# The reset gate of a GRU by seven products, with shared products added up in one PSUM bank, in a four-layer graph network

## The chip, the cores and the metric

The kernel runs on one core of one Trainium2 chip. The metric is the device time of one execution in microseconds, smaller is better. In the text PE is TensorE (the matrix engine), DVE is VectorE, ACT is ScalarE, POOL is GpSimd, and SP is SyncE, which here only issues DMAs.

## The reference, cut to what matters

The input is `x`, 128 graphs of 128 nodes with 256 features in float32, and `adj`, an integer adjacency matrix for each graph. Four layers follow one another; after each, the layer's result is added to its input and normalised over the features.

- Layer 0 is attention: four scores `(x*a_k) @ x.T`, of which `adj == k+1` picks one for each pair of nodes, a softmax, and the product with `x`.
- Layer 1 sends messages: `relu(x @ W_upd + mean over neighbours of x @ W_msg + bias)`.
- Layer 2 is a gated recurrent unit that runs three steps. This is the layer that the change concerns:

```python
m = h @ weight[i]; aggr = A.T @ m
gi = aggr @ w_ih.T + b_ih
gh = h @ w_hh.T + b_hh
r = sigmoid(i_r + h_r)            # reset gate
z = sigmoid(i_z + h_z)            # update gate
n = tanh(i_n + r * h_n)           # candidate
h = (1 - z) * n + z * h
```

- Layer 3 is attention again, with a score `f_i + f_j`, a mask `adj > 0`, a softmax and an ELU.

## The kernel before

**Tiling.** Four graphs make a group (`G = 4`), so there are 32 groups, and a tile has 128 partitions by 512 columns (four graphs of 128 nodes). The hidden state is kept transposed, in two halves `hT[0]` and `hT[1]` of 128 features each. `weight[i] @ w_ih.T` is multiplied out once, at the start, into `c_gi[:, i]`, so that a step first sums the neighbours (`aggregate`, on three bfloat16 parts of `h`), copies that to `agT`, and then multiplies by `c_gi` and `w_hhT`.

**Products of a gate.** A gate has 256 output features, 256 input features and 512 columns, from two sources (`h` with `w_hhT`, and `agT` with `c_gi`). Taken as 2 by 2 blocks it is eight block products of 256 columns for each source. `direct` does it plainly: for each half of the output, two matmuls of 512 columns for each source, all four added up in one bank. This is how the reset gate is made (lines 769 to 772), and `reset` takes its tanh from the bank. The update gate uses the seven products of the Strassen-Winograd scheme: `sums` prepares four differences of the state's blocks (`t_h` on GpSimd, `t_m` on VectorE), `w_s` holds three sums of the weights' blocks, and `seven` issues the seven products of 256 columns of a source. They lie in four banks,

```python
BANKS = ((1, 6), (5, 7), (4,), (3, 2))
```

and `gate` (line 708) adds them up into the four quarters of the tile `t_z` when all are done: one ScalarE copy, six VectorE additions, and a tanh for each half. `seven(of_h, ...)` comes ahead of `seven(of_m, ...)`, so that the products of `h` can run while the neighbours are still being summed, and the same holds for the first `direct` of each reset half.

**Order of the work.** No engine's order is written by hand. Every call is recorded as an `Op`, and a planner at the end (from line 905) issues the operations in the order of a list schedule: of those that could start first on an engine it takes the one with the smallest due time `nominal`. The due times come from `paced`, which spreads the operations of a layer over a stretch of `PERIOD` for each group; `SPAN = 2` means that the three GRU steps of a group take two periods, so two groups are always in the GRU while others are in layers 0, 1 and 3. What an operation costs the planner is in `pe_cost`, `dve_cost`, `act_cost` and `pool_cost`, what a hand-over between engines costs in `HOP`, `PE_HOP` and `SLACK`, and a landing DMA in `LANDING`. `urgent` operations (the GRU's) get `EAGER` ahead on engines other than PE. The order is fixed when the kernel is built; on the chip every engine goes through its queue in order and waits for semaphores.

**Buffers.** PSUM has four banks under the tag `ps` and four under `gate`. `t_z` and `t_h` are one buffer each, `q` and `m_gt` have three and four, `hn` (the new state turned back) has four.

**Masks and scaled inputs.** Layer 0's `prepared(k)` makes the mask `mk` on VectorE (line 534), and the scaled input `xs` for the scores half on GpSimd (line 539), half on ScalarE (line 541). Layer 1 makes `m_gt` and `a_ne` on VectorE (lines 590 to 593). Line 231, which the profile shows everywhere, is the planner's own `issue`.

Of the kernel before, what the change touches and what calls it, by code (L numbers as in the profile page):

```python
# [9 lines left out]
U8 = mybir.dt.uint8  # L10
# [8 lines left out]
def kernel(  # L19
# [135 lines left out]
    class Op:  # L155
        def __init__(self, engine):
            self.engine, self.calls, self.took, self.landing = engine, [], 0.0, 0.0
            self.after, self.bufs, self.waiting = {}, [], 0
            self.ready, self.nominal, self.urgent = 0.0, 0.0, False
            self.waits = self.holds = False  # L160

    class Engine:
        def __init__(self, name, engine, cost):
# [71 lines left out]

    LANDING = 3.8
    HOP = 0.3
    PE_HOP = 1.0  # L240
    SLACK = 1.0

    def pe_cost(op, n, sums):
        return 0.11 if op == "transpose" else 0.222 if n <= P else n / 600.0

    SPLIT = 0.056

# [51 lines left out]

    w3x = tile_of("w3x", [P, KC, 2 + D])  # L300

    w_s = tile_of("w_s", [P, NL + 1, 3, P])

    def weights():

# [2 lines left out]
        for src, tag, bufs in ((w_ih, "hT", 6), (w_hh, "rest", 4)):  # L308
            for g in range(0, NGC, 2):
                nat = tile_of(tag, [P, 2, D], bufs)  # L310
                ACT.dma_start(out=nat, in_=src[g * P : (g + 2) * P].rearrange("(g p) d -> p g d", p=P))
                nats.append(nat)
            if src is w_ih:
                for i in range(NL):
                    w = tile_of("hn", [P, KC, D], 4)
# [62 lines left out]
        for n in range(NL + 1):  # L378
            by = POOL if n > 1 else DVE
            w = [  # L380
                (w_hhT[:, k] if n == 0 else c_gi[:, n - 1, k])[:, (KC + e) * P : (KC + e + 1) * P]
                for e in range(2) for k in range(KC)
            ]
            a11, a12, a21, a22 = w
# [134 lines left out]
    def layer0(g, s):  # L519
# [11 lines left out]

        def prepared(k):
            mk = tile_of("mk", [P, G, N], 2, U8)
            DVE.tensor_scalar(mk, a_f, float(k + 1), None, op0=OP.is_equal)
            xs = []
            for c in range(KC):
                t = tile_of("xs", [P, T], 2)
                if c == 0:
                    POOL.tensor_scalar(t, xT[c], acol[:, k, c : c + 1], None, op0=OP.mult)
                else:  # L540
                    ACT.mul(t, xT[c], acol[:, k, c : c + 1])
                xs.append(t)
            return mk, xs

# [94 lines left out]
    def gru(g, s):  # L639
# [5 lines left out]
        def step(i, hT, parts):  # L645
# [31 lines left out]
            def sums(by, v, w, n, src, tag):  # L677


                t = tile_of(tag, [P, 4, H])  # L680
                b11, b12, b21, b22 = v[0][:, :H], v[0][:, H:], v[1][:, :H], v[1][:, H:]
                s12, s21, s22 = src[0][:, H:], src[1][:, :H], src[1][:, H:]
                by.tensor_sub(t[:, 0], s12, b11)
                by.tensor_sub(t[:, 2], s22, b12)
                by.tensor_sub(t[:, 1], s22, t[:, 0])
                by.tensor_sub(t[:, 3], s21, t[:, 1])
                block = lambda k, e: w[:, k, (Z + e) * P : (Z + e + 1) * P]
                return {
                    1: (block(0, 0), b11), 2: (block(1, 0), b21), 3: (w_s[:, n, 2], b22),
                    4: (block(1, 1), t[:, 3]), 5: (block(0, 1), t[:, 0]),  # L690
                    6: (w_s[:, n, 0], t[:, 1]), 7: (w_s[:, n, 1], t[:, 2]),
                }

            BANKS = ((1, 6), (5, 7), (4,), (3, 2))

            def seven(of, banks, first, last):

                for j, numbers in enumerate(BANKS):
                    if first:
                        banks.append(bank("gate"))  # L700
# [7 lines left out]
            def gate(tag, q, banks):  # L708

                t = tile_of(tag, [P, 4, H])  # L710
                b16, b57, b4, b32 = [b.rearrange("p (h n) -> p h n", [P, 2, H], h=2) for b in banks]
                ACT.copy(t[:, 0], b16[:, 0])
                DVE.tensor_add(t[:, 3], b16[:, 1], t[:, 0])
                DVE.tensor_add(t[:, 1:3], b57, t[:, 3:4].to_broadcast([P, 2, H]))
                DVE.tensor_add(t[:, 3], b57[:, 0], t[:, 2])
                DVE.tensor_add(t[:, 2], b4[:, 0], t[:, 2])
                z = [t[:, 2 * c : 2 * c + 2].rearrange("p h n -> p (h n)") for c in range(KC)]
                ACT.activation(z[1], z[1], AF.Tanh, bias=brz[:, q + 1 : q + 2], scale=0.5)
                DVE.tensor_add(t[:, 1], b32[:, 0], t[:, 1])
                DVE.tensor_add(t[:, 0], b32[:, 1], t[:, 0])  # L720
                ACT.activation(z[0], z[0], AF.Tanh, bias=brz[:, q : q + 1], scale=0.5)
                return z

            def hidden(c, ps):
                t = tile_of("q", [P, T], 3)
                ACT.activation(t, ps, AF.Identity, bias=bhn[:, c : c + 1], scale=0.5)
                return t

            def reset(c, ps):
                t = tile_of("t_r", [P, T], 2)  # L730
                ACT.activation(t, ps, AF.Tanh, bias=brz[:, c : c + 1], scale=0.5)
                return t

            def candidate(c, ps, t, q):
# [8 lines left out]
            def update(c, z, n, d):  # L743

                DVE.scalar_tensor_tensor(d, z, 1.0, d, op0=OP.add, op1=OP.mult)
                new[c] = tile_of("hT", [P, T], 6)
                DVE.scalar_tensor_tensor(new[c], d, 0.5, n, op0=OP.mult, op1=OP.add)
                turning[c] = tile_of("hn", [P, G, P], 4)
                flat = turning[c].rearrange(FLAT)
                if g == NG - 1 and i == NL - 1:  # L750
                    turned_quick(flat, [new[c][:, b * N : (b + 1) * N] for b in range(G)])
                else:
                    back(flat, turned(new[c].rearrange("p (b n) -> p b n", b=G), G, "h"))
                if i < NL - 1:
                    split_up[c] = split(turning[c], DVE)
# [131 lines left out]
    for g in range(NG):  # L887
        s = State()
        loading(g, s)
        layer0(g, s)  # L890
        paced(g - 2.0, g - 1.0)
        layer1(g, s)
        paced(g - 1.0, g - 0.05)
        gru(g, s)
        if g < NG - 1:
            layer3(g, s, 0, G)
            paced(g + SPAN + 0.05, g + SPAN + 1.0)
        else:

            for b in range(0, G, 2):  # L900
                layer3(g, s, b, b + 2)
                paced(g + SPAN + 0.05, g + SPAN + 1.0)


    order = {}
# [18 lines left out]
    def take_slot(buf):  # L924
# [6 lines left out]
    EAGER = 10.0  # L931

    def start_of(op):

# [21 lines left out]
    while left:  # L956
        best = None
        for e in engines:
# [5 lines left out]
            if best is None or at < best[0]:  # L964
                op = min(
                    (op for t, op in starts if t <= at),
                    key=lambda op: op.nominal - (EAGER if op.urgent and e is not PE else 0.0),
                )
                best = (at, op)
        at, op = best  # L970
# [50 lines left out]
```

## Time and profile before

| | |
|---|---|
| time, median of 3 runs | 2891.55 us (2890.46 to 2894.75) |
| profiled execution, span | 2889.2 us |
| PE busy | 2820.4 us, 98% |
| weight loads busy | 1814.3 us, 63% |
| DVE busy | 2418.6 us, 84% |
| ACT busy | 1277.3 us, 44% |
| POOL busy | 1293.8 us, 45% |
| mean granted TensorE clock | 0.992 |

A float32 matmul shows in the profile as two records, a bfloat16 one as one. Matmuls are pipelined: a record's end is modelled and lies beyond the start of the next, so the time that a matmul costs is read from the distance between starts. A name such as `gate<-agT,c_gi` says that a tile of the tag `gate` is written from `agT` and `c_gi`. Times in the timeline are from the start of the span.

### The profile page before, as it was taken

To read this page: it belongs to the slowest core of one execution; us is meant where nothing else is said; L and a number is where in the kernel's file an instruction comes from. 1 tells how busy PE (TensorE), PEld (TensorE's weight loads), DVE (VectorE), ACT (ScalarE), POOL (GpSimd) and SP (SyncE) were. 2 spreads that over 40 slices of the span, in tenths; PEclk is the share of its full clock that TensorE was granted. 3 is DMA by queue.
4 is the path that set the end of the run, shared out by engine and by line. 5 is a ranking of instruction groups with operands and counts; after the bars stand their busy time and mean duration, and the time that the engine had idled before them with its cause. 6 is when DMAs were issued, how large, how long until landed. Compare 5 with 4: busy or idle time off the path is not lost.

```text
span 2889.2 us, 39658 instructions
## 1 busy us (share of the span) xinstructions
PE 2820.4 (98%) x12028; PEld 1814.3 (63%) x12028; DVE 2418.6 (84%) x5549; ACT 1277.3 (44%) x2712; POOL 1293.8 (45%) x1326
## 2 busy tenths in 40 slices
PE   7799999999999999999999999999999999999996
PEld 5566666666666666666666666666666666666563
DVE  5778898888888888898888888888898888888876
ACT  3234444444444444444444444444444443444444
POOL 3434545444455444445434454444444434454432
PEclk9999999999999999999999999999999999999997
DMA  5434565555555555565555555555555555544542
GB/s 112 109 83 85 125 130 104 123 106 110 124 128 112 105 117 107 124 130 105 117 112 109 124 126 109 110 114 113 124 125 110 110 113 110 127 110 97 106 92 55
DMA packets 1396612, 321.58 MB, mean 111 GB/s; under 512 B 1142064, under 2 KB 1387952, under 8 KB 1396400
## 3 DMA queue, kind: packets, MB, share of 16 engines
q1 hardware_dynamic: 1393952, 316.69, 52.2%
q10 hardware_dynamic: 2448, 2.36, 0.3%
q8 instruction: 97, 1.59, 0.2%
q14 instruction: 115, 0.94, 0.1%
HBM read 185.74 MB, written 133.15 MB: 110 GB/s over the span
## 4 chain that ended last, share of the span: by engine, by line
PE 86%; DVE 8%; issue 3%; ACT 1%; DMA 1%; POOL 1%; SPq 0%; ACTq 0%; DVEq 0%; POOLq 0%
PE ps L231 48%; PE gate L231 38%; DVE hT L231 1%; DVE t_z L231 1%; DVE t_r L231 1%; DVE rest L231 1%; DVE t_m L231 1%; DVE st L231 1%; DVE mk L231 0%; DVE z L231 0%; DVE xd L231 0%; ACT agT L231 0%; DVE z_h L231 0%; DVE t_d L231 0%; SPq L231 0%
## 5 line engine op out<-in xcount | busy, mean ns | idle before, releaser
L231 PE MATMUL gate<-agT,c_gi 128*128 128x512 f32 (+1 forms) x1152 | 470.2, 524 | 2.7 <-ACT agT L231 2.7
L231 POOL TENSOR_TENSOR rstd<-rstd,neg_half 128x4 f32<-128x4 f32 (+1 forms) x128 | 144.7, 1131 | 512.9 <-DVE rstd L231 510.3
L231 PE MATMUL ps<-agT,c_gi 128*128 128x512 f32 x768 | 355.3, 592 | 0.0
L231 DVE TENSOR_TENSOR t_z<-gate,t_z 128x256 f32<-128x256 f32 x576 | 254.4, 460 | 86.2 <-ACT t_z L231 65.5
L231 PEld LDWEIGHTS gate<-agT,c_gi 128*128 128x128 f32 x1152 | 218.4, 191 | 160.0 <-issue 136.9
L231 PE MATMUL gate<-hT,w_hhT 128*128 128x512 f32 (+1 forms) x768 | 316.9, 530 | 0.2 <-DVE t_z L231 0.2
L231 POOL TENSOR_SCALAR xs<-xT,acol 128x512 f32<-128x512 f32 x128 | 210.3, 1643 | 205.5 <-PE ps L231 175.9
L231 PEld LDWEIGHTS ps<-xs,xT 128*128 128x128 f32 x2048 | 249.7, 193 | 66.7 <-issue 54.1
L231 PE MATMUL ps<-xs,xT 128*128 128x128 f32 x2048 | 251.5, 276 | 10.4 <-POOL xs L231 10.4
L231 ACT ACTIVATE t_n<-t_r,bih 128x512 f32<-128x512 f32 x192 | 138.0, 719 | 274.1 <-DVE t_r L231 263.3
L231 PEld LDWEIGHTS ps<-agT,c_gi 128*128 128x128 f32 x768 | 145.8, 190 | 157.4 <-issue 146.9
L231 PE MATMUL ps<-hT,w_hhT 128*128 128x512 f32 x512 | 240.8, 593 | 0.0
L231 PE MATMUL ps<-w_um,x1T 128*128 128x512 f32 x512 | 235.1, 592 | 1.9 <-ACT x1T L231 1.9
L231 ACT ACTIVATE t_r<-gate,brz 128x512 f32<-128x512 f32 x192 | 130.0, 685 | 237.5 <-PE gate L231 237.4
L231 ACT ACTIVATE t_z<-t_z,brz 128x512 f32<-128x512 f32 x192 | 131.4, 714 | 223.3 <-DVE t_z L231 220.6
L231 POOL TENSOR_TENSOR t_d<-hT,t_n 128x512 f32<-128x512 f32 x128 | 172.5, 1352 | 108.9 <-ACT t_n L231 107.3
L231 DVE TENSOR_TENSOR t_r<-t_r,ps 128x512 f32<-128x512 f32 x192 | 131.4, 685 | 98.5 <-PE ps L231 90.7
L231 POOL TENSOR_TENSOR t_d<-h0T,t_n 128x512 f32<-128x512 f32 x64 | 92.7, 1448 | 266.0 <-ACT t_n L231 266.0
L231 ACT ACTIVATE q<-ps,bhn 128x512 f32<-128x512 f32 x192 | 130.9, 682 | 173.2 <-PE ps L231 173.1
L231 PEld LDWEIGHTS gate<-hT,w_hhT 128*128 128x128 f32 x768 | 141.5, 192 | 104.5 <-issue 98.5
L231 PEld LDWEIGHTS ps<-hT,w_hhT 128*128 128x128 f32 x512 | 97.6, 191 | 108.4 <-issue 103.4
L231 ACT COPY agT<-ps 128x512 f32<-128x512 f32 x192 | 109.1, 587 | 118.7 <-PE ps L231 111.2
(191 smaller groups left out, 6249.2 us busy)
## 6 DMA issues: line engine op xcount, KB each, us to landing
way_h<-z_h SPq DMA_DIRECT2D x190, 256.0 KB, 2.4
hn<-way_h SPq DMA_DIRECT2D x760, 64.0 KB, 2.4
x_blocks<-in_x_dram SPq DMA_DIRECT2D x256, 64.0 KB, 2.3
x_in<-in_x_dram SPq DMA_DIRECT2D x32, 512.0 KB, 3.8
way_x<-xb SPq DMA_DIRECT2D x32, 512.0 KB, 3.1
way<-z SPq DMA_DIRECT2D x64, 256.0 KB, 2.5
way_p<-z_p SPq DMA_DIRECT2D x62, 256.0 KB, 2.4
probT<-way_p SPq DMA_DIRECT2D x248, 64.0 KB, 2.4
```

Source lines behind the costliest of these rows:

```text
L231: getattr(self.engine, name)(*[a.real() if isinstance(a, View) else a for a in args], **{k: a.real() if isinstance(a, View) else a for k, ...
```

## The change

The reset gate is also made from seven products of each source, with the same `t_h` and `t_m` that the update gate uses; `w_s` gets a second block of weight sums for it. `seven`, `BANKS` and the old `gate` go, and a new `gate` serves both. In it products that several quarters of the output have in common add up in one bank, `shared`: product 1, then 6, then 7, then 4. Between them ScalarE copies the bank's sum so far into a quarter of the gate's tile (`snapshot`), and the next product goes on adding to the same bank. Products 2, and then 5 and 3, lie in two other banks, and VectorE adds these to the copied quarters (`plus`); the last sum is taken by the tanh straight from the bank. Each product is added for both sources at once. A snapshot has a planner bonus of its own, `rush`.

Besides, the masks `mk` and `m_gt` go from VectorE to GpSimd, both halves of `xs` are made on ScalarE, some tiles have fewer buffers, and the planner's numbers are set anew.

```diff
-    LANDING = 3.8
+    LANDING = 4.2
...
-        return 0.11 if op == "transpose" else 0.222 if n <= P else n / 600.0
+        return 0.11 if op == "transpose" else 0.222 if n <= P else 0.003 + n / 599.0
...
-        return 0.55 if op == "memset" else 1.2 if n < 64 else 0.25 + n * 0.0023
+        return 1.56 if op in FAST else 0.55 if op == "memset" else 1.2 if n < 64 else 0.25 + n * 0.0023
...
-    PERIOD = 88.0
+    PERIOD = 92.637
     SPAN = 2.0
-    H_END, M_START, M_END = 0.25, 0.22, 0.60
+    EAGER, RUSH = 21.446, 39.26
+    L0_START, L0_END, L1_START, L1_END, L3_START, L3_END = -2.0, -1.338, -0.867, -0.05, 0.05, 1.0
+    H_END, M_START, M_END = 0.25, 0.12, 0.573
...
-    w_s = tile_of("w_s", [P, NL + 1, 3, P])
+    w_s = tile_of("w_s", [P, NL + 1, 3, 2, P])
...
             mk = tile_of("mk", [P, G, N], 2, U8)
-            DVE.tensor_scalar(mk, a_f, float(k + 1), None, op0=OP.is_equal)
+            POOL.tensor_scalar(mk, a_f, float(k + 1), None, op0=OP.is_equal)
...
-                if c == 0:
-                    POOL.tensor_scalar(t, xT[c], acol[:, k, c : c + 1], None, op0=OP.mult)
-                else:
-                    ACT.mul(t, xT[c], acol[:, k, c : c + 1])
+                ACT.mul(t, xT[c], acol[:, k, c : c + 1])
...
-        s.m_gt = tile_of("m_gt", [P, G, N], 4, U8)
-        DVE.tensor_scalar(s.m_gt, a_f, 0.0, None, op0=OP.is_gt)
+        s.m_gt = tile_of("m_gt", [P, G, N], 3, U8)
+        POOL.tensor_scalar(s.m_gt, a_f, 0.0, None, op0=OP.is_gt)
...
+            def gate(tag, q, sources):
+                t = tile_of(tag, [P, 4, H])
+                shared, other, last = bank("gate"), bank("gate"), bank("gate")
+
+                def add(ps, p, first=False):
                     with PE:
-                        for k, p in enumerate(numbers):
+                        for k, of in enumerate(sources):
                             PE.matmul(
-                                banks[j][:, k * H : (k + 1) * H], *of[p],
-                                start=(first and k == 0), stop=(last and k == len(numbers) - 1),
+                                ps[:, :H], *of(q)[p], start=(first and k == 0),
+                                stop=(p in (2, 3, 4) and k == len(sources) - 1), skip_group_check=True,
                             )
...
+                def snapshot(quarter):
+                    ACT.copy(t[:, quarter], shared[:, :H])
+                    ops[-1].rush = RUSH
+
+                def plus(quarter, ps):
+                    DVE.tensor_add(t[:, quarter], ps[:, :H], t[:, quarter])
+
+                def tanh(out, in_, c):
+                    ACT.activation(out, in_, AF.Tanh, bias=brz[:, q + c : q + c + 1], scale=0.5)
+
+                add(shared, 1, True)
+                snapshot(0)
+                add(last, 2, True)
+                plus(0, last)
+                add(shared, 6)
+                snapshot(1)
+                add(other, 5, True)
+                add(shared, 7)
+                snapshot(3)
+                plus(3, other)
+                tanh(t[:, 3], t[:, 3], 1)
+                add(shared, 4)
+                tanh(t[:, 2], shared[:, :H], 1)
+                add(other, 3)
+                plus(1, other)
+                halves = [t[:, 2 * c : 2 * c + 2].rearrange("p h n -> p (h n)") for c in range(KC)]
+                tanh(halves[0], halves[0], 0)
+                return halves[1], halves[0]
...
-                t = tile_of("q", [P, T], 3)
+                t = tile_of("q", [P, T], 2)
...
-                turning[c] = tile_of("hn", [P, G, P], 4)
+                turning[c] = tile_of("hn", [P, G, P], 3)
...
-            r0 = direct(w_hhT, hT, R, stop=False)
-            t0 = reset(0, direct(w_i, agT, R, r0))
-            r1 = direct(w_hhT, hT, R + 1, stop=False)
-            t1 = reset(1, direct(w_i, agT, R + 1, r1))
+            t1, t0 = gate("t_r", R, (of_h, of_m))
+            n1, d1 = candidate(1, direct(w_i, agT, C + 1), t1, q1)
             n0, d0 = candidate(0, direct(w_i, agT, C), t0, q0)
-            n1, d1 = candidate(1, direct(w_i, agT, C + 1), t1, q1)
-            z_banks = []
-            seven(of_h, z_banks, True, False)
-            seven(of_m, z_banks, False, True)
-            z = gate("t_z", Z, z_banks)
-            update(1, z[1], n1, d1)
-            update(0, z[0], n0, d0)
+            z1, z0 = gate("t_z", Z, (of_h, of_m))
+            update(1, z1, n1, d1)
+            update(0, z0, n0, d0)
```

More of the change, by code (lines that the diff above doesn't have):

```diff
@@ L160, in __init__ @@
             self.waits = self.holds = False
+            self.rush = 0.0
     class Engine:
@@ L314, in weights @@
                 for i in range(NL):
-                    w = tile_of("hn", [P, KC, D], 4)
+                    w = tile_of("hn", [P, KC, D], 3)
                     ACT.dma_start(out=w, in_=weight[i].rearrange("(c p) e -> p c e", p=P))
@@ L380, in weights @@
             w = [
-                (w_hhT[:, k] if n == 0 else c_gi[:, n - 1, k])[:, (KC + e) * P : (KC + e + 1) * P]
-                for e in range(2) for k in range(KC)
+                (w_hhT[:, k] if n == 0 else c_gi[:, n - 1, k])[:, : 4 * P].rearrange(
+                    "p (g e x) -> p g e x", [P, 2, 2, P], g=2, e=2
+                )
+                for k in range(KC)
             ]
-            a11, a12, a21, a22 = w
+            a11, a12, a21, a22 = w[0][:, :, 0], w[1][:, :, 0], w[0][:, :, 1], w[1][:, :, 1]
             s2, s3, s4 = [w_s[:, n, j] for j in range(3)]
@@ L686, in sums, with of @@
                 by.tensor_sub(t[:, 3], s21, t[:, 1])
[L687 to L700, printed above, removed]
+                def of(q):
+                    block = lambda k, e: w[:, k, (q + e) * P : (q + e + 1) * P]
+                    extra = lambda j: w_s[:, n, j, q // KC]
+                    return {
+                        1: (block(0, 0), b11), 2: (block(1, 0), b21), 3: (extra(2), b22),
+                        4: (block(1, 1), t[:, 3]), 5: (block(0, 1), t[:, 0]),
+                        6: (extra(0), t[:, 1]), 7: (extra(1), t[:, 2]),
+                    }
@@ L701, in seven @@
+                return of
+            def gate(tag, q, sources):
+                t = tile_of(tag, [P, 4, H])
+                shared, other, last = bank("gate"), bank("gate"), bank("gate")
+                def add(ps, p, first=False):
                     with PE:
-                        for k, p in enumerate(numbers):
+                        for k, of in enumerate(sources):
                             PE.matmul(
-                                banks[j][:, k * H : (k + 1) * H], *of[p],
-                                start=(first and k == 0), stop=(last and k == len(numbers) - 1),
-                            )
@@ L708, in gate @@
[L708 to L722, printed above, removed]
+                                ps[:, :H], *of(q)[p], start=(first and k == 0),
@@ L724, in hidden @@
+                halves = [t[:, 2 * c : 2 * c + 2].rearrange("p h n -> p (h n)") for c in range(KC)]
+                tanh(halves[0], halves[0], 0)
+                return halves[1], halves[0]
             def hidden(c, ps):
-                t = tile_of("q", [P, T], 3)
+                t = tile_of("q", [P, T], 2)
                 ACT.activation(t, ps, AF.Identity, bias=bhn[:, c : c + 1], scale=0.5)
[L727 to L731, printed above, removed]
@@ L890 @@
         layer0(g, s)
-        paced(g - 2.0, g - 1.0)
+        paced(g + L0_START, g + L0_END)
         layer1(g, s)
-        paced(g - 1.0, g - 0.05)
+        paced(g + L1_START, g + L1_END)
         gru(g, s)
@@ L896 @@
             layer3(g, s, 0, G)
-            paced(g + SPAN + 0.05, g + SPAN + 1.0)
+            paced(g + SPAN + L3_START, g + SPAN + L3_END)
         else:
@@ L901 @@
                 layer3(g, s, b, b + 2)
-                paced(g + SPAN + 0.05, g + SPAN + 1.0)
+                paced(g + SPAN + L3_START, g + SPAN + L3_END)
     order = {}
@@ L929, in take_slot @@
         taken.append(buf)
-    EAGER = 10.0
     def start_of(op):
@@ L966 @@
                     (op for t, op in starts if t <= at),
-                    key=lambda op: op.nominal - (EAGER if op.urgent and e is not PE else 0.0),
+                    key=lambda op: op.nominal - (EAGER if op.urgent and e is not PE else 0.0) - op.rush,
                 )
```

## The prediction

> **What bounds the kernel now.** I read the page's busy times first, then the chain that ended last, then the groups kept apart by shape, and last two stretches of the timeline.
>
> ```profile
> PE 2820.4 (98%) x12028; PEld 1814.3 (63%) x12028; DVE 2418.6 (84%) x5549; ACT 1277.3 (44%) x2712; POOL 1293.8 (45%) x1326
> PEclk9999999999999999999999999999999999999997
> PE 86%; DVE 8%; issue 3%; ACT 1%; DMA 1%; POOL 1%; SPq 0%; ACTq 0%; DVEq 0%; POOLq 0%
> ```
>
> PE is busy for 98% and is 86% of the chain. A busy PE can still be badly fed, so I check the spacing of its starts. In the middle of the run:
>
> ```profile
> 1401.75 1.88 PE L231 MATMUL ps<-hT,w_hhT 128*128 128x512 f32 x4
> 1403.46 1.95 PE L231 MATMUL ps<-xs,xT 128*128 128x128 f32 x16
> ...
> 1406.98 0.59 PE L231 MATMUL gate<-agT,c_gi 128*128 128x256 f32 x2
> 1407.41 0.59 PE L231 MATMUL gate<-t_m,w_s 128*128 128x256 f32 x2
> 1407.84 0.59 PE L231 MATMUL gate<-t_m,c_gi 128*128 128x256 f32 x2
> ...
> 1408.04 0.37 ACT L231 COPY t_z<-gate 128x256 f32<-128x256 f32 x1 [3.69 <-PE gate L231]
> ```
>
> Four records of 512 columns take 1403.46 - 1401.75 = 1.71 us; two records are a matmul, so 0.857 us each. A 256-column matmul takes 0.432 us (the steps 1406.98, 1407.41, 1407.84). Nothing lies between: PE streams. Between 90 and 2800 us it is busy 2689.47 of 2710.00 us in the windows view, and the waits that the trace names there come to some 30 us. So PE's own work is the time, and a matmul removed is worth its spacing unless PE begins to wait.
>
> **The skill.** The Trainium skill, "TensorE: Matmul & The Clock Gate", Back-to-back issue gap, gives N/2.4 + 2.5 ns. For 512 columns that is 216 ns; a float32 record is spaced 0.429 us, twice that, and a 256-column record 0.216 us, half of it. The trace agrees that halving the columns costs next to nothing extra. "PSUM — Partial Sum Buffer", The four PSUM rules, says that hardware allows a synchronised read of a partial sum in the middle of an accumulation group. No run so far shows it; before, every bank is read after its last product. "Perfetto Trace Analysis", Matmuls, advises that independent groups rotate through banks so that eviction overlaps the next matmuls. The shared bank does the opposite for products 6, 7 and 4, which is where a new wait could come from.
>
> **TensorE, part by part.** The reset gate was 8 matmuls of 512 columns a step: 8 x 0.857 = 6.86 us. It becomes 14 of 256: 14 x 0.432 = 6.05 us. There are 32 x 3 = 96 steps: 96 x 0.81 = 78 us off PE. The update gate keeps its 14 products, and aggregation, candidate and layers keep theirs. In the built order I count 7202 matmuls before and 7778 after, which is 96 x 6 more, as it should be.
>
> **The new wait: a shared bank between PE and ACT.** Products 6, 7 and 4 of each gate must wait until ACT has copied the bank: 3 x 2 x 96 = 576 hand-overs. Their latency can be read from before:
>
> ```profile
> 2837.34 0.28 PE L231 MATMUL ps<-a_ne,rest 128*128 128x128 bf16 x2
> 2837.65 1.07 ACT L231 COPY agT<-ps 128x512 f32<-128x512 f32 x2 [0.65 <-PE ps L231]
> 2838.29 1.13 PE L231 MATMUL gate<-agT,c_gi 128*128 128x512 f32 x2 [0.68 <-ACT agT L231]
> ```
>
> ACT starts 0.03 us after PE's modelled end, and PE starts 0.06 us after a copy of 0.58 us. For a 256-column product the end lies 0.16 us beyond the next start (0.379 against 0.216), so a hand-over needs 0.16 + 0.03 + 0.37 + 0.06 = 0.63 us of other PE work in between. I gave each matmul of the built order its spacing and summed what stands between the products of one shared bank: the median is 3.4 us before products 6 and 7 and 1.7 us before product 4. Only 3 of 576 stand with nothing between, and 13 more with 0.85 us. If ACT is prompt, this costs 3 x 0.63, about 2 us. ACT is not always prompt: behind a tanh that waits for DVE the snapshot is late, PE stops, and everything queued behind that product on PE stops with it. Before product 4 the margin is 1.7 - 0.63 = 1.1 us, one and a half ACT instructions of 0.7 us. I take 4 us in all for this, a guess between 2 and the 40 of the rival below.
>
> **The other engines.**
>
> ```profile
> L231 POOL TENSOR_SCALAR xs<-xT,acol 128x512 f32<-128x512 f32 x128 | 210.3, 1643 | 205.5 <-PE ps L231 175.9 <-DMA acol<-in_L_gnn_a_dram 11.8 <-DVE xT L231 9.8
> L231 DVE TENSOR_TENSOR t_z<-gate,t_z 128x256 f32<-128x256 f32 x480 | 188.3, 414 | 77.6 <-ACT t_z L231 65.5 <-PE gate L231 7.1 <-DVE t_z L231 0.5
> L231 DVE TENSOR_TENSOR t_z<-gate,t_z 128x512 f32<-128x512 f32 x96 | 66.2, 689 | 8.6 <-PE gate L231 0.4
> L231 DVE TENSOR_SCALAR mk<-a_f 128x512 uint8<-128x512 f32 x128 | 72.7, 571 | 1.1
> L231 DVE TENSOR_SCALAR m_gt<-a_f 128x512 uint8<-128x512 f32 x32 | 19.0, 594 | 1.4 <-POOL a_f L231 1.4
> L231 ACT ACTIVATE xs<-xT,acol 128x512 f32<-128x512 f32 x128 | 92.5, 723 | 109.4 <-PE ps L231 101.8 <-DVE xT L231 4.0 <-DVE fac L231 2.1
> L231 ACT COPY t_z<-gate 128x256 f32<-128x256 f32 x96 | 35.4, 369 | 206.2 <-PE gate L231 206.2
> ```
>
> DVE loses the masks, 72.7 + 19.0 us, and the gate additions go from 188.3 + 66.2 to 6 x 96 x 0.414 = 238 us: 2418.6 - 91.7 - 16 = 2311 us. ACT gains 128 more xs at 0.723 = 93 us, five more copies a step at 0.369 = 177 us, and a tanh of 512 columns becomes two of 256 in each of 192 gates. A 256-column tanh is not shown; the copy's 0.37 us and the 0.59 us of a 256-column scaled activation from SBUF bound it, and with 0.70 for 512 columns that is 192 x 0.04 to 192 x 0.48, or 8 to 92 us. I take 45: 1277 + 93 + 177 + 45 = 1592 us. POOL loses 210 us of xs and gains 160 masks. The trace has no mask on POOL. The skill's "GPSIMD Engine Reference", Elementwise — side-by-side cycle accounting, gives 769 ns for 512 elements, but the nearest row, also a TENSOR_SCALAR of 128x512, takes 1.643 us; I take the row, 263 us: 1294 - 210 + 263 = 1347 us, or 1207 at the page's price. In a span of 2823 us these are 82, 56 and 48%. All stay below PE, whose work hides them; PE waits for xs (10.4 us before) may fall a little, as ACT makes both halves in 1.45 us where POOL took 1.64 for one. I cost that at nothing: ACT also evicts the weights at that time. The doubled weight sums are 16 instructions once, beside PE's own 30 us of preparation. The planner's numbers and fewer buffers only move order; I cost them at nothing and leave their risk to the range.
>
> **The end.** Before, the products of h for both gates run while the last step waits for its state to come back through DRAM (PE is on them from 2824.56 to 2832.68). Now each product takes both sources at once, so all 28 stand behind the last aggregation. PE work from there: before 8 x 0.857 + 10 x 0.432 = 11.2 us, after 28 x 0.432 + 4 x 0.857 = 15.5 us, 4.3 more. Snapshots with little else queued add some 2 to 3 us, a shorter tail of additions gives 1 back. I take 6 us. In the middle of the run other groups' work fills those waits.
>
> **Sum.** 2891.5 - 78 + 4 + 6 = 2823.5, say 2823 us.
>
> **Rivals.**
> - Late snapshots. For it: ACT goes from 44 to 56% busy, in order, with waits for DVE ahead of copies. Against: the distances above, and PE waited only 7 us in all for agT copies. If a fifth of 576 hand-overs is late by 0.35 us, that is 40 us: 2859 us.
> - Slower than before. If each gate holds PE 0.5 us, through the hand-overs and a single t_r buffer together, 192 x 0.5 = 96 us: 2819 + 96 = 2915 us. The distances speak against it; a planner that is off under the new load would be for it.
> - Faster still. DVE is 108 us lighter, and PE's waits for DVE and POOL in the middle (rest 9, t_r 7, hT 5, xs 10 us) halve: 2823 - 15 = 2808 us.
> - No change: the 68 us just eaten up. Nothing points to that number.
>
> **How the numbers follow.** Forecast 0.61, late snapshots 0.20, faster still 0.12, slower 0.05, no change 0.02. The range is from just below the third rival, 2803, to just above the first, 2862, which leaves out the last two and the outer part of the others. Faster by over 0.2% is 0.61 + 0.20 + 0.12 = 0.93, same 0.01 (half of the last case), slower 0.06.
>
> **What would show it.** Right: 256-column gate matmuls still spaced 0.432 us, PE busy near 2740 us, PE's waits for ACT t_r and t_z together under 10 us, last gate matmul to the end of the span near 40 us as before. Wrong: PE idle before gate groups released by ACT t_r or t_z in tens of us, or POOL rows for mk above 2 us with DVE's alpha waiting for them.

## The result, and the profile after

The changed kernel takes 2804.52 us (median of 4 runs, 2800.18 to 2806.17); runs of the kernel before beside it gave 2893.15 us (4 runs, 2890.46 to 2895.49). The ratio is 0.9692, interval 0.9675 to 0.9708: 88.6 us less. The two profiled spans, 2889.2 and 2802.0 us, differ by 87.2 us. The forecast was 2823 us, 18.5 us too high, inside its range of 2803 to 2862.

The page of the changed kernel, busy times, the granted clock in 40 slices, and the chain that ended last by engine:

```profile
span 2802.0 us, 42709 instructions
...
PE 2741.4 (98%) x13180; PEld 2030.5 (72%) x13180; DVE 2351.3 (84%) x5389; ACT 1552.1 (55%) x3512; POOL 1349.1 (48%) x1358
...
PEclk9999999999999999999999999999999999999996
...
PE 95%; DVE 2%; ACT 1%; issue 1%; DMA 0%; POOL 0%; ACTq 0%; POOLq 0%; DVEq 0%
```

PE executes 1152 records more (two for each of 96 x 6 matmuls) and is busy 79 us less. Its share of the chain went from 86 to 95%: no wait has taken the place of the work that went. The timeline of a reset gate in the changed kernel (start, duration, engine, form, and in brackets the idle time before and who ended it):

```profile
1408.14 0.59 PE L232 MATMUL gate<-h0T,w_hhT 128*128 128x256 f32 x2
1408.58 0.59 PE L232 MATMUL gate<-agT,c_gi 128*128 128x256 f32 x2
1409.01 0.59 PE L232 MATMUL gate<-t_h,w_hhT 128*128 128x256 f32 x2
1409.44 0.59 PE L232 MATMUL gate<-t_m,c_gi 128*128 128x256 f32 x2
1409.47 0.36 ACT L232 COPY t_r<-gate 128x256 f32<-128x256 f32 x1
...
1416.32 0.59 PE L232 MATMUL gate<-t_m,w_s 128*128 128x256 f32 x2
1416.75 1.95 PE L232 MATMUL ps<-xs,xT 128*128 128x128 f32 x16
1416.95 0.37 ACT L232 COPY t_r<-gate 128x256 f32<-128x256 f32 x1 [1.04 <-PE gate L232]
1418.53 0.60 PE L232 MATMUL gate<-t_h,w_s 128*128 128x256 f32 x2
1418.96 0.59 PE L232 MATMUL gate<-t_m,w_s 128*128 128x256 f32 x2
```

The 256-column matmuls still start 0.43 us apart (1408.14, 1408.58, 1409.01, 1409.44). The sum is copied out in its middle: the product that ends at 1416.91 is copied at 1416.95, and the next one goes into the same bank at 1418.53. Between them PE does layer 0's scores (`ps<-xs,xT`), so it does not stand still. This is the read of an open accumulation that "PSUM — Partial Sum Buffer", The four PSUM rules, of the Trainium skill allows; the trace now shows 576 of them.

The view of PE's waits in the changed kernel (who waits and for what: us in all, times, longest):

```profile
PE ps L232 <- ACT wh L232: 10.8, 2, 10.0
PE ps L232 <- ACT prob L232: 6.5, 2, 4.2
PE ps L232 <- DVE hT L232: 4.8, 2, 2.9
...
PE ps L232 <- DVE rest L232: 4.5, 5, 1.8
PE gate L232 <- DVE t_z L232: 3.2, 3, 1.8
...
PE ps L232 <- ACT xs L232: 2.3, 3, 1.4
...
PE gate L232 <- ACT t_z L232: 1.4, 3, 0.5
```

The same view of the kernel before:

```profile
PE ps L231 <- POOL xs L231: 10.4, 6, 2.8
...
PE ps L231 <- DVE rest L231: 6.4, 15, 1.9
PE ps L231 <- DVE t_r L231: 5.2, 13, 0.7
```

The snapshots show there with 1.4 us (ACT `t_z`, three waits), and not at all for `t_r`. The view counts from the modelled end of the record before; from start to start the same three waits cost 1.9 us, as is worked out further down. The waits for `xs` fall from 10.4 to 2.3 us, those for DVE `t_r` vanish.

**Where 87.2 us come from.** I gave each PE record the distance that its kind has to the next when nothing is waited for (0.429 us for 512 float32 columns, 0.216 for 256, 0.1115 for 128, 0.056 for 128 in bfloat16) and put what is over in the distances between starts down as waits, apart for the first 180 us, the last 100 us and what lies between. The waits so hold more than idle time: where the granted clock falls to 0.50, as it does in parts of the first 180 and the last 100 us, records start up to twice as far apart, and that is in them too (about 6 and 7 us in the outer columns before, 5 and 8 us after). Sums in us:

| kernel | work | waits, first 180 | waits, middle | waits, last 100 | span |
|---|---|---|---|---|---|
| before | 2777.7 | 45.9 | 27.5 | 38.2 | 2889.2 |
| after | 2699.3 | 35.0 | 21.4 | 46.2 | 2802.0 |
| difference | -78.4 | -10.9 | -6.1 | +8.0 | -87.2 |

So the work fell as forecast; the waits fell by 9 where the forecast had them rise by 10. The same sums for every run below stand at the end of the experiments.

### The profile page after: what moved, and what is told of

Read it like the earlier page. It is cut to its first block, busy times and chain, and to the rows that moved or that the text cites. A ratio compares the mean times of both kernels' runs of the same rounds, so it can differ in the third digit from the quotient of the medians.

```text
span 2802.0 us, 42709 instructions
## 1 busy us (share of the span) xinstructions
PE 2741.4 (98%) x13180; PEld 2030.5 (72%) x13180; DVE 2351.3 (84%) x5389; ACT 1552.1 (55%) x3512; POOL 1349.1 (48%) x1358
## 4 chain that ended last, share of the span: by engine, by line
PE 95%; DVE 2%; ACT 1%; issue 1%; DMA 0%; POOL 0%; ACTq 0%; POOLq 0%; DVEq 0%
PE ps L232 54%; PE gate L232 41%; DVE t_r L232 0%; DVE rest L232 0%; DVE t_d L232 0%; ACT xs L232 0%; DMA acol<-in_L_gnn_a_dram 0%; DMA hn<-in_L_gnn_weight_dram 0%; ACT ps L232 0%; DVE xd L232 0%; POOL mk L232 0%; DVE hT L232 0%; DVE st L232 0%; DVE xb L232 0%; DVE t_z L232 0%
## 5 line engine op out<-in xcount | busy, mean ns | idle before, releaser
L232 PE MATMUL gate<-agT,c_gi 128*128 128x256 f32 x768 | 229.3, 380 | 1.4 <-ACT agT L232 1.4
L232 PE MATMUL gate<-t_h,w_hhT 128*128 128x256 f32 x768 | 229.0, 380 | 1.4 <-ACT t_z L232 1.4
L232 PE MATMUL gate<-t_m,c_gi 128*128 128x256 f32 x768 | 229.8, 381 | 0.0
L232 PE MATMUL gate<-t_h,w_s 128*128 128x256 f32 x768 | 228.5, 379 | 0.0
L232 PE MATMUL gate<-t_m,w_s 128*128 128x256 f32 x768 | 228.4, 379 | 0.0
L232 ACT ACTIVATE xs<-xT,acol 128x512 f32<-128x512 f32 x256 | 173.9, 715 | 64.6 <-PE ps L232 58.3
L232 POOL TENSOR_SCALAR mk<-a_f 128x512 uint8<-128x512 f32 x128 | 193.5, 1519 | 15.3 <-DVE alpha L232 9.1
L232 DVE TENSOR_TENSOR t_r<-gate,t_r 128x256 f32<-128x256 f32 x288 | 120.1, 417 | 87.0 <-PE gate L232 54.4
L232 PEld LDWEIGHTS gate<-t_h,w_s 128*128 128x128 f32 x768 | 142.8, 190 | 65.3 <-issue 48.5
L232 DVE TENSOR_TENSOR t_z<-gate,t_z 128x256 f32<-128x256 f32 x288 | 119.9, 416 | 79.0 <-PE gate L232 54.3
```

Source lines behind the costliest of these rows:

```text
L232: getattr(self.engine, name)(*[a.real() if isinstance(a, View) else a for a in args], **{k: a.real() if isinstance(a, View) else a for k, ...
```

## The experiments

My theory: the gain is PE's work for the reset gate; the rest of the change has to keep PE fed and adds nothing itself. Against it stood that moves and planner had brought most, and that snapshots or DVE's load set what could be reached. Kernels take one part out of the changed kernel, or put one part alone into the kernel before. Differences are of medians.

**The reset gate as it was, all else as changed.** Only `Z` goes through the seven products.

```diff
-            t1, t0 = gate("t_r", R, (of_h, of_m))
+            r0 = direct(w_hhT, hT, R, stop=False)
+            t0 = reset(0, direct(w_i, agT, R, r0))
+            r1 = direct(w_hhT, hT, R + 1, stop=False)
+            t1 = reset(1, direct(w_i, agT, R + 1, r1))
```

> The changed kernel, but the reset gate by eight matmuls of 512 columns again; everything else as changed. Theory (the gain is PE work): PE gets its 96 x 0.81 = 78 us back, so 2804.5 + 78 = 2882 us, at most 15 us either way for the waits. Rival (most of the gain is the masks and the new planner numbers, and the seven products only fill waits): below 2850 us.

Measured: 2884.0 us, ratio to before 0.9974 (0.9965 to 0.9982); 79.5 us over the changed kernel. Its page:

```profile
PE 2820.2 (98%) x12028; PEld 1807.6 (63%) x12028; DVE 2219.0 (77%) x5101; ACT 1450.2 (50%) x3128; POOL 1346.0 (47%) x1358
```

PE's busy time is back at 2820 us, and by the sums above all of the 77.8 us between the spans is work (2777.7 against 2699.3; waits 102.1 against 102.6). The theory holds: one part of the change is worth 79.5 of the 88.6 us. This kernel is still 7 us faster than the kernel before beside it: that is what is left of the change, and its waits in the first 180 us are 34.6 against 45.9 us.

**Masks back on DVE, half of `xs` back on GpSimd.**

```diff
-            POOL.tensor_scalar(mk, a_f, float(k + 1), None, op0=OP.is_equal)
+            DVE.tensor_scalar(mk, a_f, float(k + 1), None, op0=OP.is_equal)
...
-                ACT.mul(t, xT[c], acol[:, k, c : c + 1])
+                if c == 0:
+                    POOL.tensor_scalar(t, xT[c], acol[:, k, c : c + 1], None, op0=OP.mult)
+                else:
+                    ACT.mul(t, xT[c], acol[:, k, c : c + 1])
...
-        POOL.tensor_scalar(s.m_gt, a_f, 0.0, None, op0=OP.is_gt)
+        DVE.tensor_scalar(s.m_gt, a_f, 0.0, None, op0=OP.is_gt)
```

> The changed kernel, but mk and m_gt on VectorE and half of xs on GpSimd, as before. DVE gets about 90 us more work, some 87% of the span. Theory: PE stays the bound, and the time is 2804 to 2815 us. Rival (the moves are what keeps DVE from holding PE up): 2825 us or more, with PE waits for DVE in the middle of the run.

Measured: 2874.85 us, ratio 0.9944 (0.9931 to 0.9956), 70 us over the changed kernel; the theory's number is missed. PE's waits:

```profile
PE gate L232 <- ACT t_z L232: 26.8, 58, 0.5
PE gate L232 <- DVE t_z L232: 21.1, 27, 1.3
PE ps L232 <- ACT wh L232: 10.2, 2, 9.4
PE ps L232 <- POOL xs L232: 7.5, 5, 2.6
```

Here are the hand-over waits that I had been afraid of: 58 of some 0.46 us for the copy of `t_z`. They are not slow copies. In this kernel's queue product 4 stands directly behind product 7 in 58 of 192 gates; in the changed kernel's in 3, and that one has 3 such waits. The planner, given other work on DVE and GpSimd, wrote another order. So this run mixes load and order, and the number alone would have misled. The frozen order further down takes out one part of the load.

**The planner's numbers as before** (`LANDING`, the matmul's cost, `PERIOD`, `EAGER`, the stretches, no `RUSH`), and **no `RUSH` alone**:

```diff
-    EAGER, RUSH = 21.446, 39.26
+    EAGER, RUSH = 21.446, 0.0
```

> The changed kernel with the planner's numbers of before (LANDING, PERIOD, EAGER, the stretches, no rush; the cost of masks on GpSimd stays). Theory: the order is what gave the 17 us fewer waits at the head and in the middle, so 2815 to 2830 us. Rival A (the numbers do not matter): 2800 to 2810 us. Rival B (with the old order the snapshots stop PE): 2850 us or more, with PE waits for ACT t_r and t_z of tens of us.

> The changed kernel without the planner bonus of the snapshots (RUSH = 0). Theory (hand-overs have margin): within 8 us of 2804.5. Rival (the snapshots must come first on ScalarE or PE stops): 2820 us or more.

Measured: 2855.14 us, 0.9878 (0.9865 to 0.9892), and 2853.33 us, 0.9874 (0.9859 to 0.9889): 51 and 49 us over the changed kernel. Neither theory's number held; those of the rivals (2850 or more, 2820 or more) came instead. With the old numbers hand-overs show in PE's waits (ACT `t_z` 17.2 us in 23 waits). Without `RUSH` they hardly do; the waits are elsewhere:

```profile
PE ps L232 <- ACT wh L232: 23.0, 4, 11.7
PE ps L232 <- DVE t_m L232: 10.4, 8, 1.3
PE ps L232 <- DVE rest L232: 8.5, 14, 1.8
```

So taking `RUSH` away did not make the snapshots late; it made another order. That called for a control: how far does any other order move the time?

**Two controls.** A number of the planner is moved by a few per cent, with the operations and their engines untouched: the mask's cost from 1.56 to 1.50, and `LANDING` from 4.2 to 4.0.

```diff
-        return 1.56 if op in FAST else 0.55 if op == "memset" else 1.2 if n < 64 else 0.25 + n * 0.0023
+        return 1.50 if op in FAST else 0.55 if op == "memset" else 1.2 if n < 64 else 0.25 + n * 0.0023
```

> A control: the changed kernel with the same operations on the same engines, but the planner told that a mask on GpSimd takes 1.50 us where it is told 1.56 (the trace has 1.52). The order comes out different on every engine, the work does not. Theory A (the 70, 51 and 49 us lost by the masks back, the old numbers and no rush belong to those edits): 2800 to 2812 us. Theory B (most of those losses is the loss of an order that suits this one list of operations, and any new order loses it): 2825 to 2860 us.

> A second control: the changed kernel with LANDING = 4.0 where it is 4.2 (before it was 3.8); nothing else. Theory A: 2800 to 2812 us. Theory B: 2825 to 2860 us, with PE waits spread over ACT and DVE in the middle of the run.

Measured: 2837.18 us, 0.9811 (0.9796 to 0.9826), and 2817.97 us, 0.9746 (0.9731 to 0.9760): 33 and 13.5 us over the changed kernel, the first as Theory B had it, the second between the two. The first waits once for 10.6 us on a landing of `hn`, the second nine times on DVE `alpha`, 10.9 us. Moving one planned cost by 0.06 us costs 33 us (the trace has 1.52 us for it, between the two values). So an order drawn anew costs 13.5 and 33 us here without any reason in the operations. The 49 and 51 us above are larger than both, but two controls don't bound what an order can cost, so these losses can't be put down to `RUSH` or to the other numbers as such: all that these do is choose an order.

**The moves alone, on the kernel before**, and **moves with the new planner's numbers on the kernel before** (the same edits of masks, `xs` and the masks' cost; the second also takes `LANDING`, the matmul's cost, `PERIOD`, `EAGER` and the stretches).

```diff
-    PERIOD = 88.0
+    PERIOD = 92.637
...
-    H_END, M_START, M_END = 0.25, 0.22, 0.60
+    EAGER = 21.446
+    L0_START, L0_END, L1_START, L1_END, L3_START, L3_END = -2.0, -1.338, -0.867, -0.05, 0.05, 1.0
+    H_END, M_START, M_END = 0.25, 0.12, 0.573
```

> The kernel before with only mk and m_gt moved to GpSimd and both halves of xs to ScalarE (and the planner told the GpSimd price). PE's work is that of before. If the moves are worth something by themselves, it is at most the waits that PE had for DVE and xs: 2870 to 2885 us. If a new order alone costs time (theory B): 2900 to 2940 us. If neither: 2886 to 2898 us.

> The kernel before with the moves and all the new planner numbers, but the reset gate and the update gate as before. With the reset gate's 78 us of PE work still there, the theory says 2875 to 2895 us. If the moves and numbers bring most of the gain by themselves: below 2850 us. If the numbers suit only the changed list of operations: above 2900 us.

Measured: 2890.8 us, 0.9999 (0.9990 to 1.0008), and 3049.83 us, 1.0546 (1.0531 to 1.0562). In the first, waits of the first 180 us fall from 45.9 to 35.6 us and those in the middle rise from 27.5 to 38.6: the moves do quicken the start, and are lost again later. In the second one wait for the layer 1 result comes back in 27 of the 32 groups. Here are the sum of these waits, one of them in the timeline, and the engines' busy time and the granted clock (`PEclk`) right after it:

```profile
PE ps L231 <- DVE hu L231: 116.3, 27, 4.8
```

```profile
603.77 6.64 PE L231 MATMUL ps<-h0T,w_hhT 128*128 128x512 f32 x8 [4.29 <-DVE hu L231]
```

```profile
core 0: us, PE busy (x) PEld busy (x) DVE busy (x) ACT busy (x) POOL busy (x), PEclk, DMA share, GB/s
604.00:609.00 5.00, 5.00 (x6) 1.92 (x7) 2.40 (x6) 1.44 (x3) 0.41 (x1) 0.50 0.36 57
```

Each of the 27 waits, 3.9 to 4.8 us long, goes with a stretch of 3.4 or 6.8 us at a granted clock of 0.50. The eight records after this one take 6.64 us, where the same eight take 3.60 us at full clock (at 2832.68 in the kernel before). Over the middle of the run these stretches add about 55 us to the 116.3 us of the waits themselves, so a long wait here costs about half as much again as its length.

Neither the moves, nor the moves and the numbers, make the kernel before faster. The direct reset gate by itself is not what the new numbers don't suit: the first run of this section has it, with these numbers and the new update gate, at 2884.0 us. What in the kernel before makes PE wait for layer 1 under them, no run parts.

**The same order, masks on DVE.** To part load from order I let the planner reckon with the mask on GpSimd, but issue it on DVE at the place where DVE's queue would have it. The queues of PE, ACT and SP are the changed kernel's, instruction for instruction. `by` is a field added to the recorded operation, and the planner's `issue` uses it as the engine.

```diff
             POOL.tensor_scalar(mk, a_f, float(k + 1), None, op0=OP.is_equal)
+            ops[-1].by = nc.vector
...
         POOL.tensor_scalar(s.m_gt, a_f, 0.0, None, op0=OP.is_gt)
+        ops[-1].by = nc.vector
```

> The changed kernel in its own order: the planner still plans mk and m_gt as GpSimd work at GpSimd's price, but they are issued on VectorE, at the same place among the other operations. TensorE, ScalarE and SyncE have the same instructions in the same order as in the changed kernel. DVE gets 160 masks, about 90 us. Theory (the order cost 70 us in the run with the masks back, not DVE's load): 2800 to 2815 us. Rival (DVE's load is what counts; moving the masks off it was needed): 2830 us or more, with PE waits for DVE.

Measured: 2825.88 us, 0.9773 (0.9759 to 0.9788), 21 us over the changed kernel, between the two. PE's waits and the mask's group:

```profile
PE ps L233 <- DVE t_r L233: 9.9, 12, 0.8
...
PE ps L233 <- DVE rest L233: 7.5, 18, 1.7
```

```profile
L233 DVE TENSOR_SCALAR mk<-a_f 128x512 uint8<-128x512 f32 x128 | 56.4, 441 | 0.2
```

With DVE at 85% PE begins to wait for DVE's results. The masks on DVE, with GpSimd freed of them, cost 21 us in this order. If that holds in the other order too, which isn't shown, 49 of the 70 us above are the order and `xs`, which I did not part further.

**The same order, every snapshot copied twice.** The planner reckons with one copy, so all other queues stay. It adds up to one copy, 0.37 us, to each hand-over.

```diff
-                    ACT.copy(t[:, quarter], shared[:, :H])
+                    with ACT:
+                        ACT.copy(t[:, quarter], shared[:, :H])
+                        ACT.copy(t[:, quarter], shared[:, :H])
+                    ops[-1].took /= 2
```

> The changed kernel in its own order, but each snapshot is copied twice on ScalarE in a row, while the planner reckons with one; every other queue is the same. Each hand-over is 0.37 us later and needs 1.0 us of other PE work in place of 0.63, and ACT gets 576 x 0.37 = 213 us more. Theory (the order leaves margin; 16 of 576 hand-overs have under 1.0 us): 2805 to 2815 us. Rival (hand-overs sit at the edge): 2830 us or more, with PE waits for ACT t_r and t_z.

Measured: 2815.62 us, 0.9738 (0.9723 to 0.9752), 11 us over the changed kernel and 0.6 us above what the theory allowed; ACT is 62% busy, and waits in the middle rise by 9 us. ACT's busy time rises by 184 us (from 1552.1 to 1736.4; copies in a row overlap a little), of which 11 us, a seventeenth, reach the end. The margin of the hand-overs in this order is measured, not only argued.

**The end.** In the changed kernel the last 100 us wait 8 us more. Its timeline there:

```profile
2726.47 0.59 PE L232 MATMUL gate<-agT,w_s 128*128 128x256 f32 x2
2737.06 5.75 PE L232 MATMUL ps<-hT,w_hhT 128*128 128x512 f32 x8 [9.99 <-ACT wh L232]
...
2743.98 0.65 PE L232 MATMUL gate<-hT,w_hhT 128*128 128x256 f32 x2
...
2757.85 0.59 PE L232 MATMUL gate<-t_m,w_s 128*128 128x256 f32 x2
2758.91 0.70 PE L232 MATMUL gate<-t_h,w_hhT 128*128 128x256 f32 x2 [0.46 <-ACT t_z L232]
...
2761.31 0.89 PE L232 MATMUL gate<-hT,w_s 128*128 128x256 f32 x2 [1.27 <-DVE t_z L232]
2762.00 1.06 PE L232 MATMUL gate<-agT,w_s 128*128 128x256 f32 x2
```

PE stands for 9.99 us ahead of the candidate's products of `h`, because their `ps` bank is held until ACT has copied layer 3's `wh`. I gave them a bank of `gate` in the last step of the last group, which is free there.

```diff
-                ps = ps or bank("ps" if q >= C else "gate")
+                ps = ps or bank("ps" if q >= C and not (tail and v is hT) else "gate")
```

> The changed kernel, but in the last step of the last group the two products for q take banks of the tag gate in place of ps. In the trace PE stands still for 9.99 us there, ended by ACT wh. Theory (it waits for a ps bank that the layer 3 products hold until ACT has read them): that wait falls to some 3 us and the time to 2796 to 2800 us. Rival (it waits for the state itself, or what is saved there is lost at the landing of hn right after): 2802 to 2806 us.

Measured: 2803.55 us, 0.9697 (0.9681 to 0.9713): no difference from the changed kernel. Its timeline:

```profile
2732.03 5.14 PE L232 MATMUL gate<-hT,w_hhT 128*128 128x512 f32 x8 [4.48 <-DVE hT L232]
...
2738.31 0.22 PE L232 MATMUL ps<-a_ne,hn 128*128 128x128 bf16 x1 [1.14 <-ACT wh L232]
...
2740.32 0.23 PE L232 MATMUL ps<-a_ne,rest 128*128 128x128 bf16 x1 [1.79 <-DVE rest L232]
...
2743.45 1.17 PE L232 MATMUL gate<-hT,w_hhT 128*128 128x256 f32 x2
```

The wait for the bank was real: the products now start 5.0 us earlier (2732.03 against 2737.06). But PE then waits for ACT `wh` again and for `rest`, which is made from the state that comes back through DRAM (`hn`), and the gates behind the aggregation start only 0.5 us earlier (2743.45 against 2743.98). The rival is right: the end is a chain of dependencies, and a wait on it is not a cause just because it is the longest.

**Other numbers for the planner, as a try for a faster order** (the changed operations throughout):

```diff
-    LANDING = 4.2
+    LANDING = 4.15
...
-    EAGER, RUSH = 21.446, 39.26
-    L0_START, L0_END, L1_START, L1_END, L3_START, L3_END = -2.0, -1.338, -0.867, -0.05, 0.05, 1.0
-    H_END, M_START, M_END = 0.25, 0.12, 0.573
+    EAGER, RUSH = 16.381, 28.172
+    L0_START, L0_END, L1_START, L1_END, L3_START, L3_END = -2.0, -1.338, -0.837, -0.05, 0.05, 1.0
+    H_END, M_START, M_END = 0.244, 0.182, 0.574
```

> The changed kernel with the same operations on the same engines and six of the planner's numbers set otherwise (LANDING 4.15, EAGER 16.381, RUSH 28.172, L1_START -0.837, H_END 0.244, M_START 0.182), taken because the planner's own schedule ends earliest with them among some hundreds of settings. PE's work is the same 2699 us of spacings. Theory (what a new order costs or brings lies in PE's waits in the middle of the run, of which the changed kernel has only 21 us): no better than 2785 us, likely 2785 to 2805 us. Rival (any order but the one that was found loses, as the two controls did): 2812 to 2850 us.

Measured: 2799.81 us, 0.9686 (0.9670 to 0.9702), the lowest median of all; its interval covers the changed kernel's ratio, so it isn't shown to be faster. Waits in the middle are 21.0 against 21.4 us. There is little left there for an order to gain.

The sums of PE's work and waits for these runs, in us, as in the table above:

| kernel | work | first 180 | middle | last 100 | span |
|---|---|---|---|---|---|
| reset gate as it was | 2777.7 | 34.6 | 26.3 | 41.2 | 2879.8 |
| masks and xs back | 2699.3 | 42.1 | 85.4 | 47.2 | 2873.9 |
| planner as before | 2699.3 | 40.4 | 70.9 | 42.3 | 2852.9 |
| no RUSH | 2699.3 | 34.9 | 70.1 | 46.7 | 2851.0 |
| mask's cost 1.50 | 2699.3 | 37.3 | 52.6 | 46.9 | 2836.1 |
| LANDING 4.0 | 2699.3 | 38.4 | 32.3 | 48.3 | 2818.3 |
| before with moves | 2777.7 | 35.6 | 38.6 | 37.4 | 2889.2 |
| before with moves and numbers | 2777.7 | 30.5 | 194.3 | 41.4 | 3043.9 |
| masks on DVE, same order | 2699.3 | 37.7 | 41.2 | 46.0 | 2824.3 |
| copies twice, same order | 2699.3 | 35.5 | 30.3 | 47.8 | 2813.0 |
| gate bank at the end | 2699.3 | 35.7 | 20.9 | 45.7 | 2801.6 |
| other numbers | 2699.3 | 33.3 | 21.0 | 44.2 | 2797.8 |

Work takes two values only, with or without the seven products of the reset gate. Everything else is waits, and what the lower granted clock adds to them, above all in the middle.

## Why the prediction was right, and where it was off

- **TensorE, -78 us: right.** -78.4 us by the spacings, and 77.8 and 79.5 us come back when it alone is undone (span and median). The spacing stayed 0.43 us, PE busy came to 2741.4 us where "near 2740" was said.
- **The shared bank, +4 us: right, in this order.** The hand-over was read rightly. Where nothing stands between, product 4 starts 1.06 us after the product before it (2758.91 against 2757.85), and with its own spacing of 0.43 us taken off that is 0.63 us, as forecast. The three of them make 1.9 us, where "3 x 0.63, about 2 us" was said. The other 2 us, for a late ACT, did not come, and doubling every copy costs 11 us. The distances that the forecast rested on belong to the order and not to the code: in the order that went with the masks on DVE, 58 hand-overs have nothing between and cost 26.8 us in the view, or 58 x 0.63 = 36 us from start to start. That is the number of the rival "late snapshots", through products that stand too close and not through late copies, and the step of counting distances in the built order was what ruled it out here.
- **The end, +6 us: +8.0 measured.** Last gate matmul to the end of the span is 39 us (from about 2763), as said. PE's longest wait there was for a bank, which the forecast had not seen, but behind that bank lay the last step's chain, as the run with the `gate` bank shows.
- **The mis-sized term: PE's other waits, "I cost that at nothing".** They fell: 10.9 us at the start and 6.1 us in the middle. At the start it is the moves: put alone into the kernel before, they take 10.3 us of waits there (45.9 to 35.6), and taken out of the changed kernel they put 7.1 us back (35.0 to 42.1). Waits for `xs` are most of what goes from the list. The forecast had named these and put them at nothing because ACT evicts the weights at that time; the runs do not bear that reason out. For the middle the frozen order shows only that DVE's load can matter there: the masks put 20 us back. That the lighter DVE is what took the 6.1 us is argued, since the moves alone raise the middle of the kernel before by 11 us (27.5 to 38.6). About 18 us less here in place of nothing, 2 us less for the snapshots and 1 to 2 us more at the end come to some 19 us, against the 18.5 by which the forecast was too high. The number is thus nearer to that of the rival "faster still", 2808 us, but that rival had misread where the waits lie: the six for `xs` all come before 135 us and those for `hT` at 121 us or after 2824 us, so in the middle of the kernel before the list has only `t_r` with 5.2 us and `rest` with 3.0 us.
- **The planner's numbers "only move order; I cost them at nothing": right for this pair by luck, and wrong as a reason.** Order is worth 13 to 51 us with the same work, and 159 us where the new numbers meet the kernel before; the changed kernel's order is among the best of those run, which suggests that the numbers were fitted to this list of operations. A forecast can't take that from the diff; the range ought to have named it as the main risk, more than late snapshots.
- **The other engines.** DVE 2351 against 2311 forecast, ACT 1552 against 1592, POOL 1349 against 1347. All lay under PE. A part of DVE's excess, 18 us, is the row `t_d<-t_z,t_d`, 691 ns before and 781 now; it is 788 in the same order without masks on GpSimd, so these don't stretch it there. What does can be read from the trace: 62 of the 192 start while GpSimd is in a TENSOR_TENSOR and take 1.00 us in the mean, the other 130 take 0.68; before, 2 of 192 start so. Of the two bounds for the mask on GpSimd the row's was right: 1.519 us measured, 1.643 taken.

Open too: the kernel with the direct reset gate was planned anew from the same numbers and lost nothing in waits, while each new order of the changed kernel, but for the one with the numbers of the last run, lost 13 us or more. DVE at 77% busy in the first and 84% in the second could be why; no run tests it.

## What to carry to other kernels

Where PE streams for 98% of the span, price a removed matmul at its start-to-start spacing, and find what stands between each new pair of dependent instructions in the order as built: a hand-over cost 0.63 us with nothing between, and with 0.87 us of other PE work between, as ahead of 13 of the products 4, the list of waits doesn't show it. A group's mean can mix two kinds of instruction, so single ones are worth reading against what the other engines do just then. Where a schedule is fitted to its operations, an edit's loss is not the edit's until a control with another order, or the same queues held fixed, says so. The longest wait at the end of a chain is worth nothing if what it waited for would have been followed by another.

## What was not expected of the hardware

- **A mask on VectorE is held while GpSimd is in a TENSOR_TENSOR; beside a TENSOR_SCALAR it mostly isn't.** In the mean one mask took 0.571 us before, 0.441 us in the run with the order held, and 0.550 us in the run with masks and `xs` back:

```profile
L232 DVE TENSOR_SCALAR mk<-a_f 128x512 uint8<-128x512 f32 x128 | 69.9, 550 | 1.0
```

  The half of `xs` on GpSimd looks like the cause, but single instructions of that last run say otherwise:

```profile
1343.08 1.27 POOL L232 TENSOR_TENSOR rT<-rT,hT 128x512 f32<-128x512 f32 x1 [0.63 <-DVE hT L232]
1343.67 0.96 DVE L232 TENSOR_SCALAR mk<-a_f 128x512 uint8<-128x512 f32 x1
...
1349.16 1.67 POOL L232 TENSOR_SCALAR xs<-xT,acol 128x512 f32<-128x512 f32 x1 [2.17 <-PE ps L232]
1349.95 0.42 DVE L232 TENSOR_SCALAR mk<-a_f 128x512 uint8<-128x512 f32 x1
```

  The first mask ends at 1344.63, 0.28 us after GpSimd's TENSOR_TENSOR (1344.35). Of 31 masks that start inside such an instruction 30 end 0.28 to 0.29 us after it and take 0.47 to 1.49 us, which makes up all of what the mean is above 0.42 us; in the kernel before 32 of 32 end so. The 54 masks that lie wholly inside an `xs` take 0.42 us in the mean, as with GpSimd idle; only 2 that start in the last 0.3 us of one are held to 0.28 us after its end. So the mean follows from how many masks the order puts beside a TENSOR_TENSOR. It fits the Trainium skill, "GPSIMD Engine Reference", Key points, by which GpSimd shares its interfaces to SBUF with VectorE and the two contend in some modes; which of them is at work here isn't shown.
- **Opening a sum in its middle is cheap.** Of 576 reads of an unfinished bank by ACT, with PE adding to it afterwards, the list of waits names 3, those with no other PE work between; from start to start they cost 0.63 us each.
